# Rebuilding the first stages of a product-quantised convolution block and issuing three lookups ahead of the numerators

## The chip, the cores and the metric

The kernel runs on one core of one Trainium2 chip. The metric is the device time of one execution in microseconds (us), median over runs. Ratios are computed as the mean time of one kernel's runs over that of the other's of the same rounds, so they are not quite the ratios of the medians quoted.

## The reference, cut to what matters

x is 16 images of 256 channels of 28 x 28, fp32. Twice in a row each channel's 3 x 3 patches are compared with 16 centroids, and a softmax over them weighs a table of 256 outputs:

```python
def amm_conv3x3(x, centroids, w_sub):
    p = patches(x)                                    # B, 784, C, 9
    d = sum(p*p) - 2*einsum('bncs,cks->bnck', p, centroids) + sum(centroids**2)
    attn = softmax(-d)                                # over 16 centroids
    lut = einsum('cks,cso->cko', centroids, w_sub)
    return einsum('bnck,cko->bno', attn, lut)

out = relu(bn1(amm_conv3x3(groupnorm(x), centroids1, wsub1)))
out = se(bn2(amm_conv3x3(out, centroids2, wsub2)))
return x + relu(out + groupnorm(x))
```

## The kernel before: the parts that the change and the argument touch

The work is 512 steps: 16 images x 2 layers x 2 halves of the pixels (384 and 400) x 8 groups of 32 channels. A step has these parts: **logits** (16 small matmuls of patches and codes on TensorE), **exponentials** (two activations on ScalarE), **numerators** (16 small matmuls), two **transposes** and a reciprocal on VectorE, the product with the reciprocal on GpSimd, one more transpose, and, three steps later, the **lookups** (matmuls of 128 x 128 with the sub-weights; 36 for 8 steps). Patches come from DRAM: each normalised image is written there in nine shifted copies and read back as rows.

Eight PSUM banks are two accumulators and three pairs that rotate:

```python
def pair():
    turn[0] += 1
    return ring[turn[0] % 3]

def logits(u, rows):
    ps = [pair(), pair()]
    for t in range(4):
        for i in range(4):
            nc.tensor.matmul(ps[t // 2][...], lhsT=wd..., rhs=u["pt"]..., ...)

def b_exp(u):      # ScalarE: two activations of 2 x 400
    for ps in u.pop("lg"):
        nc.scalar.activation(e[:, :, :n], ps[:, :, :n], AF.Exp, scale=2.0)

def b_num(u):
    u["nm"] = [pair(), pair()]
    ...            # t = 0, 1 need the first exponential, t = 2, 3 the second

def b_turn(u):     # VectorE: frees the numerators' pairs
    for v, ps in enumerate(u.pop("nm")):
        nc.vector.transpose(nt[...2 * v...], ps[...])
    nc.vector.reciprocal(rc[...], u["nt"][:, :, SUM])
```

A pair is two banks, and holds half of a group's results. Four pairs are taken per step and three exist. If a step's logits have pairs a and b, its numerators have c and a, and the next logits have b and c. So the **second half of the next logits waits for the first transpose of this step's numerators**.

Within a step the order on every engine is by position:

```python
LOGITS, LOAD, MOVE, EXP, LOOK_A, NUM, TURN, SMALL, LOOK_B, MAX, LOOK_C, TURN_BACK, REST = range(13)
...
for i, (m, o, h) in enumerate(LOOKS[k : k + n]):
    self.at(s, LOOK_A if i < n // 2 + n % 2 - more[q] // 2 else LOOK_B if i < n - more[q] else LOOK_C, c_look, ...)
```

n is 4 or 5; it is 2 more in steps in which an extra group of logits for a maximum is made (position MAX). SMALL holds tiny matmuls of the group statistics and of the gate.

Before the loop, image 0 is normalised and written out. The channels are sorted by an estimate of their range, and the first layer's sub-weights are sorted with them on TensorE. The second layer's tables are sorted during the first steps.

## Time and profile before

| | before |
|---|---|
| median of 3 runs | 2973.09 us (2972.99 to 2977.15) |
| span of the profiled run | 2969.2 us |
| TensorE idle in the first 80 us | 47.1 us |
| first logits | 57.0 us |
| numerators after two lookups, width 384 / 400 | 1.04 / 1.19 us |
| logits of the same size | 0.86 / 0.88 us |

A start-to-start distance (from a group's start to the next group's) is the right measure of a group here, since a busy TensorE is not one at its peak. Two lines of the list of waits of the kernel before (who waited for whom: us in total, times, longest) name the wait that the numerators have and the one that logits nearly never had. L631 are the numerators, L563 the logits, PEld is the weight load in front of a matmul.

```profile
PEld pair L631 <- ACT e L621: 321.4, 555, 7.1
...
PEld pair L563 <- DVE nt L643: 7.4, 11, 1.2
```

The totals are idle time of the weight loads. Most of it overlaps matmuls, so the counts tell more than the microseconds: 555 waits for exponentials against 11 for transposes.

### The profile page before, as it was taken

What the parts mean: (1) busy time and instruction counts of PE and PEld (TensorE: products, weight loads), DVE (VectorE), ACT (ScalarE), POOL (GpSimd) and SP (SyncE); (2) the same over time, 40 slices, a digit from 0 to 9 for tenths busy, and PEclk for the clock granted to TensorE, in tenths of its full rate; (3) what the DMA queues carried; (4) which work ended last, traced back from release to release, by engine and by line L of the source; (5) the groups of instructions that cost most, each with busy time, mean ns of one, the idle gap of its engine ahead of it and who ended that gap; (6) DMA issues with size and microseconds to landing.
All of it is one profiled execution on the core that took longest, in us unless ns stands there. A gap on an engine that the chain in (4) does not pass through costs nothing.

```text
span 2969.2 us, 94838 instructions
## 1 busy us (share of the span) xinstructions
PE 2871.6 (97%) x39834; PEld 1145.4 (39%) x39834; DVE 2252.7 (76%) x2760; ACT 1092.7 (37%) x1605; POOL 1768.5 (60%) x2583
## 2 busy tenths in 40 slices
PE   4999999999999999999999999999999999999995
PEld 2433333333333333333333333333333333334332
DVE  3476777787877878787787877878788787878884
ACT  1332343433434343343433434343343434333332
POOL 3474575666656566665656656566665656656553
PEclk8999999999999999999999999999999999999998
DMA  6877777767767676776767667676776767674641
GB/s 185 227 174 170 203 219 195 212 154 213 186 169 197 151 208 174 197 185 154 211 156 207 180 180 188 154 214 156 214 185 163 200 155 206 177 189 106 163 114 56
DMA packets 296773, 530.30 MB, mean 179 GB/s; under 512 B 94240, under 2 KB 251664, under 8 KB 296336
## 3 DMA queue, kind: packets, MB, share of 16 engines
q0 software_dynamic: 51648, 269.78, 34.9%
q1 hardware_dynamic: 242512, 251.70, 32.7%
q8 instruction: 316, 5.18, 0.7%
q10 hardware_dynamic: 2176, 2.65, 0.3%
q14 instruction: 121, 0.99, 0.1%
HBM read 269.96 MB, written 254.05 MB: 176 GB/s over the span
## 4 chain that ended last, share of the span: by engine, by line
PE 79%; DMA 7%; DVE 6%; POOL 4%; issue 2%; ACT 2%; SPq 0%; ACTq 0%; DVEq 0%; POOLq 0%
PE acc L695 47%; PE pair L631 16%; PE pair L563 14%; DMA xt<-in_x 4%; DVE nt L643 2%; POOL k L659 2%; DVE rc L649 1%; DVE gn_st L417 1%; POOL total L671 1%; DMA pt<-pat 1%; ACT e L621 1%; DMA ws<-dws 1%; PE pair L309 0%; PE pair L324 0%; DVE q L677 0%
## 5 line engine op out<-in xcount | busy, mean ns | idle before, releaser
L695 PE MATMUL acc<-q,ws 128*128 128x384 f32 (+1 forms) x4096 | 1641.0, 519 | 9.7 <-ACT y L717 9.7
L659 POOL TENSOR_TENSOR k<-nt,rc 128x832 f32<-128x832 f32 (+1 forms) x512 | 802.3, 1567 | 1132.9 <-DVE rc L649 1120.5
L643 DVE STREAM_TRANSPOSE nt<-pair 128x832 f32<-128x832 f32 (+1 forms) x1024 | 976.3, 992 | 603.5 <-PE pair L631 506.4
L621 ACT ACTIVATE e<-pair 128x800 f32<-128x800 f32 (+1 forms) x1024 | 787.8, 821 | 1358.8 <-PE pair L563 1357.3
L695 PEld LDWEIGHTS acc<-q,ws 128*128 128x128 f32 x4096 | 696.9, 189 | 907.7 <-issue 577.2
L631 PE MATMUL pair<-e,cw 32*32 32x384 f32 (+1 forms) x16384 | 580.3, 502 | 11.9 <-ACT e L621 10.6
L563 PE MATMUL pair<-pt,wd 19*32 19x384 f32 (+2 forms) x18432 | 561.0, 500 | 5.9 <-DMA pt<-pat 3.3
L677 DVE STREAM_TRANSPOSE q<-k 128x832 f32<-128x832 f32 (+1 forms) x512 | 489.1, 955 | 0.8 <-POOL k L659 0.8
L649 DVE RECIPROCAL rc<-nt 128x104 f32<-128x104 f32 (+1 forms) x512 | 398.5, 778 | 17.6
L631 PEld LDWEIGHTS pair<-e,cw 32*32 32x32 f32 x16384 | 167.5, 103 | 349.2 <-ACT e L621 321.4
L563 PEld LDWEIGHTS pair<-pt,wd 19*32 19x32 f32 (+1 forms) x18432 | 138.4, 103 | 340.1 <-issue 265.5
L665 POOL TENSOR_TENSOR tail<-nt,rc 128x104 f32<-128x104 f32 (+1 forms) x512 | 242.4, 473 | 0.0
L695 PE MATMUL acc<-qt,ws 128*128 128x400 f32 (+1 forms) x512 | 218.6, 509 | 0.0
L671 POOL TENSOR_TENSOR total<-total,nt 128x96 f32<-128x96 f32 (+1 forms) x448 | 198.7, 443 | 0.0
L468 POOL DMA_DIRECT2D pat<-side x280 | 186.6, 667 | 1.1 <-DMA pat<-im 0.7
L671 POOL TENSOR_TENSOR total<-total,rc 128x96 f32<-128x96 f32 (+1 forms) x448 | 175.5, 392 | 0.0
L695 PEld LDWEIGHTS acc<-qt,ws 128*128 128x128 f32 x512 | 90.8, 189 | 100.1 <-issue 50.6
L587 DVE TENSOR_REDUCE mx<-z 128x48 f32<-128x768 f32 (+1 forms) x128 | 120.8, 943 | 0.0
L582 DVE STREAM_TRANSPOSE z<-pair 128x768 f32<-128x768 f32 (+1 forms) x128 | 119.2, 969 | 0.0
L468 POOL DMA_DIRECT2D pat<-im x140 | 94.0, 672 | 3.5 <-ACT im L447 3.5
L707 ACT ACTIVATE im<-acc,bnsh,bnsc 128x384 f32<-128x384 f32 (+1 forms) x64 | 43.4, 678 | 139.4 <-PE acc L695 133.4
L717 ACT ACTIVATE y<-acc,bnsh,bnsc 128x384 f32<-128x384 f32 (+1 forms) x64 | 43.4, 679 | 91.7 <-PE acc L695 76.8
(106 smaller groups left out, 753.5 us busy)
## 6 DMA issues: line engine op xcount, KB each, us to landing
pat<-side POOLq DMA_DIRECT2D x232, 588.0 KB, 6.1
pt<-pat SPq DMA_DIRECT2D x1024, 112.5 KB
pt<-pat SPq DMA_DIRECT2D x1024, 108.0 KB
pat<-im POOLq DMA_DIRECT2D x116, 588.0 KB, 5.3
xt<-in_x POOLq DMA_DIRECT2D x32, 784.0 KB, 8.8
out_dram<-y POOLq DMA_DIRECT2D x16, 784.0 KB, 4.0
pat<-side POOLq DMA_DIRECT2D x24, 300.0 KB, 6.1
pat<-side POOLq DMA_DIRECT2D x24, 288.0 KB, 6.0
```

Source lines behind the costliest of these rows:

```text
L468: nc.gpsimd.dma_start(view(pat, (ROWS * p0 + 9 * k + 3 * dx) * HW + px, [[ROWS * HW, m], [HW, 3], [1, n]]), bass.AP(v.tensor, v.offset, [l ...
L563: nc.tensor.matmul(ps[t // 2][c : c + 32, t % 2, :n], lhsT=wd[l][32 * i : 32 * i + rows, 4 * u["m"] + t, :], rhs=u["pt"][32 * i : 32 * i + ...
L587: nc.vector.tensor_reduce(u["mx"][:, 2 * v : 2 * v + 2].rearrange("p t (j b) -> p t b j", j=2)[:, :, :nb], u["z"].pop(0)[:, : 64 * nb].rea ...
L621: nc.scalar.activation(e[:, :, :n], ps[:, :, :n], AF.Exp, scale=2.0)
L631: nc.tensor.matmul(u["nm"][t // 2][32 * i : 32 * i + 32, t % 2, :n], lhsT=cw[l][c : c + 32, 4 * u["m"] + t, :], rhs=es[t // 2][c : c + 32, ...
L643: nc.vector.transpose(nt[:, :nb, 2 * v : 2 * v + 2].rearrange("p b t r -> p t b r"), ps[:, :, : 32 * nb].rearrange("p t (b r) -> p t b r", ...
L649: nc.vector.reciprocal(rc[:, : 8 * nb], u["nt"][:, :, SUM])
L659: nc.gpsimd.tensor_tensor(q[:, :nb].rearrange("p b (a s) -> p (b a) s", s=8), nt[:, :, :8], rc.unsqueeze(2).to_broadcast([P, 8 * nb, 8]), ...
L665: nc.gpsimd.tensor_tensor(tails[key][:, :nb, 8 * (m % 4) : 8 * (m % 4) + 8], nt[:, :, 8].rearrange("p (b a) -> p b a", a=8), rc.rearrange( ...
L671: nc.gpsimd.tensor_add(t[:, : 8 * nb], t[:, : 8 * nb], v)
L677: nc.vector.transpose(q[:, :, : 32 * nb].rearrange("p h (b r) -> p h b r", r=32), u.pop("k")[:, :nb].rearrange("p b (h r) -> p h b r", h=2),)
L695: nc.tensor.matmul(accs[key][:, :n], lhsT=ws[l][:, 2 * m + h if h < 2 else 2 * NQ + m // 4, o * P : (o + 1) * P], rhs=u["q"][h][:, :n], st ...
```

## The change

Its intent is to start the loop earlier and to give the exponentials time for one more lookup before the numerators need them. The channel sort moves to where x loads. The first layer's sub-weights are loaded at once into three of the six patch buffers. Patch writes go by the first half of the channels, then the second. The second layer's sorted sub-weights are copied by VectorE, and its sorted tables (codes and sub-weights) are stored by GpSimd. In the loop, three lookups always go ahead of the numerators.

```diff
+    raw = [t.rearrange("p a n -> p (a n)")[:, :1536]... for t in pts[3:]]
+    for i in range(NLT * P // PART):
+        nc.sync.dma_start(raw[i // 2][:, i % 2], ws1[:, i * PART : (i + 1) * PART]...)
...
-            nc.scalar.dma_start(view(d_c2[i], ...), t)
+            nc.gpsimd.dma_start(view(d_c2[i], ...), t)
...
-        nc.scalar.copy(r, ps[:, :, :PART])
-        nc.scalar.dma_start(view(d_ws2, ...), r)
+        nc.vector.tensor_copy(r, ps[:, :, :PART])
+        nc.gpsimd.dma_start(view(d_ws2, ...), r)
...
-    STEPS = [(dx, k, h) for dx in (1, 0, 2) for k in range(NB) for h in range(2)]
+    STEPS = [(dx, k, h) for h in range(2) for dx in (1, 0, 2) for k in range(NB)]
...
-                        self.at(s, LOOK_A if i < n // 2 + n % 2 - more[q] // 2 else LOOK_B if i < n - more[q] else LOOK_C, c_look, of[m], o, h)
+                        self.at(s, LOOK_A if i < 3 else LOOK_B if i < n - more[q] else LOOK_C, c_look, of[m], o, h)
...
-                    self.at(t + 4 * i + 2 + k, REST, shift, l, dx, k)
+                    self.at(t + (2 * i + k if pace == 1 else i), REST, shift, l, dx, k)
...
+    bn_setup()
+    row = sort_keys()
+    square_codes(0)
     for k in range(NB):
         gn_stats(0, k)
     gn_mean(0)
     gn_var(0)
+    sort_ranks(row)
+    setup_codes(0)
...
-            n0 = -3 if b == 1 else t - 2 * NS - 3
+            n0 = 2 if b == 1 else t - 2 * NS - 3
```

Cut here: the order of loads, the second issuer (SyncE) of the first patch writes, the arithmetic of the slots of the patch writes, and the removal of what moved.

More of the change, by code (lines that the diff above doesn't have):

```diff
@@ L24 @@
 NQ = NT // 4
+PART = 384
 NLT = NQ * 9 // 4
@@ L150 @@
     load_x(0, x[0])
-    pts = [const.tile([P, 4, 400], F32, name=f"pt{i}") for i in range(6)]
-    for t in pts:
-        nc.sync.dma_start(t[ONE::32], view(consts, 0, [[0, 4], [0, 4], [1, 400]]))
     def load(ap, name):
@@ L163 @@
     vecs = load(vec, "vecs")
-    nhalf_sb = load(nhalf, "nhalf_sb")
-    mones_sb = const.tile([P, 2, 32], F32, name="mones_sb")
-    nc.sync.dma_start(mones_sb, mones.rearrange("l p m -> p l m"))
     c2_sb = const.tile([P, NB, K * 9], F32, name="c2_sb")
@@ L177, with ones_row @@
     perm = sort_sb[:, n_in : n_in + NB * C].rearrange("p (b c) -> p b c", b=NB)
+    nhalf_sb = load(nhalf, "nhalf_sb")
     wd = [load(wd1, "wd0"), const.tile([P, NT, 32], F32, name="wd1")]
+    mones_sb = const.tile([P, 2, 32], F32, name="mones_sb")
+    nc.sync.dma_start(mones_sb, mones.rearrange("l p m -> p l m"))
+    pts = [const.tile([P, 4, 400], F32, name=f"pt{i}") for i in range(6)]
+    def ones_row(t):
+        nc.sync.dma_start(t[ONE::32], view(consts, 0, [[0, 4], [0, 4], [1, 400]]))
+    for t in pts[:3]:
+        ones_row(t)
+    raw = [t.rearrange("p a n -> p (a n)")[:, :1536].rearrange("p (i b m) -> p i b m", i=2, b=NB) for t in pts[3:]]
+    for i in range(NLT * P // PART):
+        nc.sync.dma_start(raw[i // 2][:, i % 2], ws1[:, i * PART : (i + 1) * PART].rearrange("(b p) m -> p b m", p=P))
     cw = [load(cw1, "cw0"), load(cw2, "cw1")]
@@ L240, in scratch, with sort_keys @@
         return kpool.tile([P, 13, 64], F32, tag="k", name="scratch").rearrange("p i m -> p (i m)")[:, :n]
-    def sort_channels():
+    def sort_keys():
         sc, sh = bn[0]
@@ L263, in sort_channels, with sort_ranks @@
         nc.vector.tensor_copy(row, ps[:, :C])
+        return row
+    def sort_ranks(row):
         own = small.tile([P, NB], F32, name="key_own")
@@ L292, in sort_bn @@
             nc.vector.tensor_copy(bn[0][i], ps[:, i : 2 * NB : 2])
-    PART = 384
     parts = {}
@@ L303, in sort_ws1 @@
     def sort_ws1(i):
-        t = parts.pop(i)
+        t = raw[i // 2][:, i % 2]
         for j in range(PART // P):
@@ L339, in sort_c2 @@
                 )
-            nc.scalar.dma_start(view(d_c2[i], 0, [[K * 9, P], [P * K * 9, NB], [1, K * 9]]), t)
+            nc.gpsimd.dma_start(view(d_c2[i], 0, [[K * 9, P], [P * K * 9, NB], [1, K * 9]]), t)
     def sort_ws2(i):
@@ L346, in sort_ws2 @@
         r = tpool.tile([P, 832], F32, tag="z", name="part")[:, : NB * PART].rearrange("p (b m) -> p b m", b=NB)
-        nc.scalar.copy(r, ps[:, :, :PART])
-        nc.scalar.dma_start(view(d_ws2, i * PART, [[9 * C, P], [P * 9 * C, NB], [1, PART]]), r)
+        nc.vector.tensor_copy(r, ps[:, :, :PART])
+        nc.gpsimd.dma_start(view(d_ws2, i * PART, [[9 * C, P], [P * 9 * C, NB], [1, PART]]), r)
     def place_wd2(j, s):
@@ L459, in shift, with to_pat @@
             nc.scalar.copy(to[:, :, 0 : W - 1], img[:, :, 1:W])
-    STEPS = [(dx, k, h) for dx in (1, 0, 2) for k in range(NB) for h in range(2)]
-    def to_pat(l, i, pat, px=0, n=HW):
+    STEPS = [(dx, k, h) for h in range(2) for dx in (1, 0, 2) for k in range(NB)]
+    def to_pat(l, i, pat, px=0, n=HW, eng=nc.gpsimd):
         dx, k, h = STEPS[i]
@@ L467, in to_pat @@
         v = (ims[l] if dx == 1 else sides[dx])[p0 : p0 + m, k, px:]
-        nc.gpsimd.dma_start(
+        eng.dma_start(
             view(pat, (ROWS * p0 + 9 * k + 3 * dx) * HW + px, [[ROWS * HW, m], [HW, 3], [1, n]]),
@@ L791, in stage, with prep, prep_near @@
                 self.tiles.append((n0, of))
-        def prep(self, l, pat, t):
+        def prep(self, l, pat, t, pace=1):
             for i, dx in enumerate((0, 2)):
                 for k in range(NB):
-                    self.at(t + 4 * i + 2 + k, REST, shift, l, dx, k)
+                    self.at(t + (2 * i + k if pace == 1 else i), REST, shift, l, dx, k)
             for i in range(len(STEPS)):
-                self.at(t + i, REST, to_pat, l, i, pat)
-        def prep_near(self, l, pat, t, slots, t2, slots2):
+                self.at(t + int(i * pace), REST, to_pat, l, i, pat)
+        def prep_near(self, l, pat, t):
             for i, dx in enumerate((0, 2)):
@@ L805, in prep_near @@
                     self.at(t + i, REST, shift, l, dx, k)
-            for i in range(len(STEPS)):
-                self.at(t + i * slots // len(STEPS), REST, to_pat, l, i, pat, *PXT[0])
-                self.at(t2 + i * slots2 // len(STEPS), REST, to_pat, l, i, pat, *PXT[1])
+            n = len(STEPS) // 2
+            for i, (dx, k, h) in enumerate(STEPS):
+                self.at(t + i // 2, REST, to_pat, l, i, pat, *PXT[0])
+                self.at(t + 6 if dx == 1 else t + 7 + 3 * h + (i - n * h - NB) * 3 // 4, REST, to_pat, l, i, pat, *PXT[1])
         def norm(self, b, t):
@@ L847 @@
             shift(0, dx, k)
-        to_pat(0, i, d_pat[0], *PXT[0])
-    square_codes(0)
-    setup_codes(0)
-    bn_setup()
-    sort_channels()
+        to_pat(0, i, d_pat[0], *PXT[0], eng=nc.gpsimd if dx == 0 or (dx, h) == (1, 1) else nc.sync)
     sort_bn()
@@ L859 @@
         if l == 0 and b >= 1:
-            n0 = -3 if b == 1 else t - 2 * NS - 3
-            plan.at(n0 - 2, REST, load_x, b, x[b])
+            n0 = 2 if b == 1 else t - 2 * NS - 3
+            plan.at(n0 - (6 if b == 1 else 2), REST, load_x, b, x[b])
             plan.norm(b, n0)
-            plan.prep(0, pat_of(0, b), {1: 1, 2: 32, 3: 56}.get(b, t - 2 * NS + 3))
+            plan.prep(0, pat_of(0, b), {1: 8, 2: 33, 3: 57}.get(b, t - 2 * NS + 3), 0.7 if b == 1 else 1)
         if l == 1:
             if b in (0, B - 1):
-                t0 = t - NS + LC
-                plan.prep_near(1, pat_of(1, b), t0, 4, t0 + 4, 8)
+                plan.prep_near(1, pat_of(1, b), t - NS + LC)
             else:
-                plan.prep(1, pat_of(1, b), 44 if b == 1 else t - 2 * NS + LC + 1)
+                plan.prep(1, pat_of(1, b), 45 if b == 1 else t - 2 * NS + LC + 1)
             plan.at(t + NS, REST, load_x, b, x[b])
@@ L872 @@
     for i in range(len(STEPS)):
-        plan.at(i // 3, REST, to_pat, 0, i, d_pat[0], *PXT[1])
-    n1 = NLT * P // PART
-    for i in range(n1):
-        if i < 2:
-            plan.at(-6, REST, load_part, ws1, i)
-            plan.at(-1, REST, sort_ws1, i)
-        else:
-            plan.at((i - 2) * 3 // 4 - 1, REST, load_part, ws1, i)
-            plan.at((i - 2) * 3 // 4, (LOOK_A, LOOK_B)[i % 2], sort_ws1, i)
+        plan.at(i * 5 // len(STEPS), REST, to_pat, 0, i, d_pat[0], *PXT[1])
+    for i in range(NLT * P // PART):
+        plan.at((i - 2) // 2, REST if i < 2 else (LOOK_A, LOOK_B)[i % 2], sort_ws1, i)
+        if i % 2:
+            plan.at((i - 2) // 2, REST, ones_row, pts[3 + i // 2])
     plan.at(3, REST, sort_c2)
```

## The prediction

> **What bounds the kernel now.** I read the profile's first two parts, then the table of stretches, then TensorE's instructions in order of time, early and in the middle.
>
> ```profile
> PE 2871.6 (97%) x39834; PEld 1145.4 (39%) x39834; DVE 2252.7 (76%) x2760; ACT 1092.7 (37%) x1605; POOL 1768.5 (60%) x2583
> ```
>
> TensorE is busy for all but 2969.2 - 2871.6 = 97.6 us. The stretches of the start (length, then busy time and count for each engine, granted clock, DMA share, GB/s) say where nearly half of that lies:
>
> ```profile
> 0.00:20.00 20.00, 1.17 (x4) 1.00 (x4) 4.11 (x22) 5.12 (x8) 7.13 (x21) 1.00 0.57 174
> 20.00:40.00 20.00, 4.97 (x10) 2.76 (x10) 8.43 (x28) 1.34 (x2) 10.22 (x17) 0.85 0.90 273
> 40.00:60.00 20.00, 13.72 (x75) 10.78 (x76) 6.45 (x21) 3.43 (x8) 0.38 (x2) 0.63 0.44 108
> 60.00:80.00 20.00, 13.03 (x190) 6.78 (x189) 7.18 (x11) 5.86 (x11) 10.96 (x20) 0.88 0.77 199
> 80.00:100.00 20.00, 19.61 (x215) 9.90 (x207) 11.22 (x14) 7.58 (x12) 13.26 (x22) 0.95 0.90 252
> ```
>
> TensorE does 32.9 us in the first 80, so it idles 47.1. The first logits start at 57.01. They wait behind one serial chain: statistics of x at 9.8, patch writes from 17.8, the code squares behind those writes in GpSimd's order (26.3), VectorE's channel sort (33.5 to 43.1), the statistics of the second batch (45.4), then 8.34 us of sub-weight sorting on TensorE. At the end 9.7 us are one wait of the last stage for the previous output's store, and some 21 us are the tail. Both stay.
>
> The rest is a steady loop of 512 steps, one for four matmul groups: 16 logits, lookups, 16 numerators, lookups. A timeline of TensorE in it (start, us, line, count; fp32 matmuls are counted twice, so x4 is two lookups):
>
> ```profile
> 1516.05 0.93 PE L563 MATMUL pair<-pt,wd 21*32 21x384 f32 x32
> 1516.91 1.61 PE L695 MATMUL acc<-q,ws 128*128 128x400 f32 x4
> 1518.45 1.08 PE L631 MATMUL pair<-e,cw 32*32 32x384 f32 x32
> 1519.47 1.61 PE L695 MATMUL acc<-q,ws 128*128 128x400 f32 x4
> 1521.01 0.93 PE L563 MATMUL pair<-pt,wd 19*32 19x384 f32 x32
> ```
>
> From one group's start to the next: logits 0.86, two lookups 1.54, numerators 1.02. Logits and numerators have the same size, so the numerators lose 0.16 here. I took this distance for all groups between 400 and 2880 us. Where two lookups stand ahead and nothing special happens, numerators take 1.04 at width 384 (106 groups) and 1.19 at 400 (115); where three stand ahead, mostly 0.86 and 0.88. The exponentials explain it: ScalarE starts 1.04 us after the logits' start and needs 0.75 to 0.83 each for two, so the second ends 0.1 to 0.3 us after the numerators have started. This loss is counted as busy.
>
> **What the Trainium skill says.** "Perfetto Trace Analysis", section "Identifying the Most-Contended Engine", says that matmul busy time is no good measure of the distance to the roofline. This trace agrees: the 97% contain the numerators' loss of some 0.24 us per affected step. "TensorE: Matmul & The Clock Gate", section "Architectural detail: the array is 16× 32×32, not 1× 128×128", gives TensorE a queue in which weight loads are pulled ahead of running matmuls, while ScalarE and VectorE are strict FIFO. The trace agrees in what a wait costs: if the second half of a group is released late, the whole half, 0.84 us, follows the release instead of half of 0.88. One case in full:
>
> ```profile
> 890.13 0.90 PE L563 MATMUL pair<-pt,wd 19*32 19x400 f32 x16
> 890.29 1.94 DVE L643 STREAM_TRANSPOSE nt<-pair 128x832 f32<-128x832 f32 x2
> 891.35 0.91 PE L563 MATMUL pair<-pt,wd 19*32 19x400 f32 x16 [0.32 <-DVE nt L643]
> 892.18 1.27 PE L695 MATMUL acc<-q,ws 128*128 128x400 f32 x3
> ```
>
> The first transpose ends at 890.29 + 0.97 = 891.26, 1.13 after the logits' start; the group takes 2.05. The logits that were held by a transpose ending 0.37, 0.43, 0.47, 0.61, 1.00 and 1.13 after their start took 1.30, 1.37, 1.39, 1.53, 1.92 and 2.05. So a group takes (release after its start) + 0.93, and at least 0.86 to 0.88. Lastly "DMA: Bandwidth & Descriptors", section "Issuing engines are not separate DMA queues", says that all issuers share the same 16 engines; splitting the writes over two issuers therefore saves issue time (0.65 us each on GpSimd here), not bandwidth.
>
> **The change, part by part.**
> (1) *Start.* The sort's keys run while x loads, the ranks during the normalisation, the squares before it. From the durations in the trace: x lands at about 10, but its statistics now stand behind the keys on VectorE (3.8 us of work plus a 0.45 MB load), so I put them at 12.5 to 14.7; normalised x at 20 (16.5 to 18.5 before); ranks 15 to 21, code setup to 24, sort of the batch norm to 26; sub-weight sorting 26 to 33 because the weights are already in patch buffers. Patch writes start at 20, and the first patches need only the first half of channels, 1.8 of 3.5 MB. But 2.4 MB of sub-weights now load before, about 8 us at the 273 to 340 GB/s seen at this place; so the first patches land at about 33. First logits at 34 instead of 57: -23. Steps 0 to 3 took 57 to 84 us with two stalls, 6.4 us on ScalarE (held by normalising batch 1, which now moves to steps 6 and 7) and about 2 on VectorE; I take -6 for them and give 2 back to crowded DMA (share 0.90 at 80 to 100). Sum: -27 us.
> (2) *Weight copies and their DMA issues* go from ScalarE to VectorE and GpSimd: six of under 1 us, beside other work, 0.
> (3) *Three lookups ahead.* By the loop's plan a pair of stages (32 steps) has 22 steps with four lookups, 2 of four lookups plus two that go with a maximum, and 8 that had three ahead already. So 352 and 32 steps change from 2+2 to 3+1, and from 2+2+2 to 3+1+2. About 40 of the 352 have a tiny matmul of the statistics or of the gate in between and neither gain nor lose much, leaving 310.
>  Gain: the numerators' excess goes: 1.04 - 0.86 = 0.18 and 1.19 - 0.885 = 0.305, mean 0.24.
>  Loss: three PSUM pairs rotate, four are taken per step, so the second half of the next logits gets the numerators' first pair, and must wait until VectorE has transposed it. That transpose starts 1.05 (384) or 1.08 (400) after the numerators' start, with two and with three lookups ahead alike, and lasts 0.93 or 0.99: released at 1.98 or 2.07. With two lookups behind, the logits start at about 2.6: free. With one they start at 0.86 + 0.745 = 1.60 or 0.88 + 0.77 = 1.65; the release comes 0.38 or 0.42 after, so they take 1.31 or 1.35 instead of 0.86 or 0.88: +0.46.
>  Net 310 x (0.46 - 0.24) = +68. In the 32 maximum steps the extra logits lose the 0.46, and the logits after them wait for the first maximum transpose (ends 4.75 after the numerators' start, they start at about 4.5: +0.27): 32 x (0.73 - 0.24) = +16. Sum +84, of which I take 3 as hidden in the crowded first stage: +81.
> Total: 2973 - 27 + 81 = 3027 us, 1.8% slower.
>
> **Rivals.**
> (a) The wait on the transpose does not replace the wait on the exponential, say because the logits' start moves for another reason. Then 310 + 32 steps gain 0.24, -82, and with the start -109: 2864 us. For it: steps with three ahead show numerators at the floor. Against it: all those have two lookups behind, so they say nothing of one behind; and the rotation and the six releases above are direct.
> (b) The start gains nearly nothing, since DMA becomes its bound: bytes up to 100 us are 20.1 MB at a mean of 201 GB/s, and the share is 0.90 at 20 to 40. Then 3045 to 3054 us. Against it: the DMA share is 0.44 at 40 to 60, when TensorE sorts, so there is room.
> (c) VectorE, 76% busy, becomes the bound in steps with maxima: its backlog starts the transpose later than 1.08 (1.35 in a tenth of steps), adding up to 0.3 to a tenth of 310, +9: 3036.
>
> **Range and chances.** Rival (a) I give 8%; it is the only way to faster by over 2% (under 2914). Otherwise start -15 to -33 and loop +60 to +100 give 3000 to 3058 about 3027. The limit of slower by over 2% is 3033, just above my middle, hence 39%.
>
> **What would show it.** Right: first logits near 34 us; numerators at 0.86 to 0.88 after three lookups; logits after a single lookup at 1.3 to 1.35, with TensorE waiting for the transposes into nt; waits of numerators for the exponentials gone. Wrong: logits still at 0.88 (then a), first logits after 45 (then b), transposes starting more than 1.1 after the numerators (then c).

## The result, and the profile after

The changed kernel takes **3014.0 us** (median of 3, 3012.25 to 3018.08) against 2973.09. The ratio is 1.0136, interval 1.0113 to 1.0159. So it is 41 us, 1.4%, slower, which counts as the same within 2%. The prediction said 3027, 54 us slower, with a range of 3000 to 3058.

In the changed kernel's source the lines are 10 further down: L573 logits, L641 numerators, L653 the transposes, L705 lookups. The same stretches of the start as the prediction shows for before (length, busy time and count of PE, PEld, DVE, ACT, POOL, granted clock, DMA share, GB/s):

```profile
0.00:20.00 20.00, 2.75 (x9) 2.28 (x10) 12.96 (x54) 1.60 (x3) 8.06 (x21) 1.00 0.86 278
20.00:40.00 20.00, 11.27 (x38) 8.06 (x37) 4.06 (x10) 6.34 (x10) 5.99 (x11) 0.83 0.77 187
40.00:60.00 20.00, 15.68 (x148) 8.67 (x164) 3.73 (x6) 5.02 (x10) 4.41 (x7) 0.74 0.49 143
60.00:80.00 20.00, 18.92 (x266) 9.16 (x235) 15.23 (x22) 6.39 (x12) 13.88 (x22) 1.00 0.87 236
80.00:100.00 20.00, 15.98 (x165) 7.26 (x165) 10.33 (x13) 4.22 (x6) 12.62 (x23) 0.95 0.65 180
```

TensorE is busy 48.6 us of the first 80 instead of 32.9: VectorE now sorts in the first 20 us (12.96 busy, 4.11 before). But from 80 to 100 TensorE stands for 4.0 us, before for 0.4. The first logits start at 44.22 us instead of 57.01:

```profile
44.22 3.72 PE L573 MATMUL pair<-pt,wd 19*32 19x384 f32 x32 [10.80 <-issue]
```

The loop, in order of time, TensorE and VectorE (start, us, line, count):

```profile
1545.86 0.93 PE L641 MATMUL pair<-e,cw 32*32 32x384 f32 x32
1546.72 0.91 PE L705 MATMUL acc<-q,ws 128*128 128x384 f32 x2
1546.91 1.85 DVE L653 STREAM_TRANSPOSE nt<-pair 128x768 f32<-128x768 f32 x2 [2.26 <-PE pair L641]
1547.56 1.27 PE L573 MATMUL pair<-pt,wd 21*32 21x384 f32 x32
1548.76 2.20 PE L705 MATMUL acc<-q,ws 128*128 128x384 f32 x6
...
1550.89 0.93 PE L641 MATMUL pair<-e,cw 32*32 32x384 f32 x32
```

Read the distances: numerators 0.86 (1.02 in the prediction's excerpt), one lookup 0.84, logits 1.20 (0.86 before), three lookups 2.13. The first transpose ends at 1546.91 + 0.92 = 1547.83, that is 0.27 after the logits' start, and 0.27 + 0.93 = 1.20. The weight loads of those logits name the reason in brackets:

```profile
1547.56 0.18 PEld L573 LDWEIGHTS pair<-pt,wd 21*32 21x32 f32 x16 [0.55 <-DMA pt<-pat]
1547.95 0.18 PEld L573 LDWEIGHTS pair<-pt,wd 21*32 21x32 f32 x16 [0.21 <-DVE nt L653]
```

The second 16 weight loads start only after the transpose. The list of waits turned round accordingly:

```profile
PEld pair L573 <- DVE nt L653: 95.8, 340, 2.2
PEld pair L641 <- ACT e L631: 88.9, 158, 1.7
```

Logits waited for transposes 340 times instead of 11, numerators for exponentials 158 times instead of 555.

**Where the time went.** VectorE makes one reciprocal per step, so their 512 start times in each trace align the two runs step by step. Changed minus before: -9.0 us at step 0, -17.0 at step 4, -9.6 at step 7, -10.5 at step 16; then it rises steadily, to -1.2 at step 128, +9.6 at 256, +23.1 at 384, and +40.6 at the last step. So the start (here up to step 16) gained 10.5 us, and the loop lost 51.1 us over 495 steps.

### The profile page after: what moved, and what is told of

Its sections match the earlier page's. It is cut to its first block, busy times and chain, and to the rows that moved or that the text cites. A ratio compares the mean times of both kernels' runs of the same rounds, so it can differ in the third digit from the quotient of the medians.

```text
span 3010.4 us, 94911 instructions
## 1 busy us (share of the span) xinstructions
PE 2908.8 (97%) x39834; PEld 1148.4 (38%) x39834; DVE 2258.3 (75%) x2766; ACT 1095.1 (36%) x1599; POOL 1767.6 (59%) x2585
## 4 chain that ended last, share of the span: by engine, by line
PE 87%; DMA 4%; POOL 3%; DVE 3%; issue 2%; SPq 0%; ACT 0%; DVEq 0%; POOLq 0%; ACTq 0%
PE acc L705 52%; PE pair L573 20%; PE pair L641 14%; DMA xt<-in_x 3%; POOL k L669 1%; DVE nt L653 1%; POOL total L681 1%; DVE rc L659 1%; PE pair L319 1%; PE pair L334 1%; POOL tail L675 0%; DVE gn_st L427 0%; DMA pt<-dm 0%; DMA pat<-im 0%; PE pair L506 0%
## 5 line engine op out<-in xcount | busy, mean ns | idle before, releaser
L705 PE MATMUL acc<-q,ws 128*128 128x384 f32 (+1 forms) x4096 | 1647.7, 521 | 17.1 <-ACT y L727 9.8
L653 DVE STREAM_TRANSPOSE nt<-pair 128x832 f32<-128x832 f32 (+1 forms) x1024 | 977.2, 992 | 635.0 <-PE pair L641 461.6
L705 PEld LDWEIGHTS acc<-q,ws 128*128 128x128 f32 x4096 | 695.7, 190 | 927.5 <-issue 589.8
L573 PE MATMUL pair<-pt,wd 19*32 19x384 f32 (+2 forms) x18432 | 690.3, 501 | 22.9 <-issue 10.8
L641 PE MATMUL pair<-e,cw 32*32 32x384 f32 (+1 forms) x16384 | 487.1, 500 | 1.0 <-ACT e L631 1.0
L573 PEld LDWEIGHTS pair<-pt,wd 19*32 19x32 f32 (+1 forms) x18432 | 187.0, 103 | 437.6 <-issue 256.6
L641 PEld LDWEIGHTS pair<-e,cw 32*32 32x32 f32 x16384 | 121.3, 103 | 289.9 <-issue 176.2
L705 PE MATMUL acc<-qt,ws 128*128 128x400 f32 (+1 forms) x512 | 215.0, 502 | 0.0
L705 PEld LDWEIGHTS acc<-qt,ws 128*128 128x128 f32 x512 | 93.6, 190 | 88.3 <-issue 28.9
```

Source lines behind the costliest of these rows:

```text
L573: nc.tensor.matmul(ps[t // 2][c : c + 32, t % 2, :n], lhsT=wd[l][32 * i : 32 * i + rows, 4 * u["m"] + t, :], rhs=u["pt"][32 * i : 32 * i + ...
L641: nc.tensor.matmul(u["nm"][t // 2][32 * i : 32 * i + 32, t % 2, :n], lhsT=cw[l][c : c + 32, 4 * u["m"] + t, :], rhs=es[t // 2][c : c + 32, ...
L653: nc.vector.transpose(nt[:, :nb, 2 * v : 2 * v + 2].rearrange("p b t r -> p t b r"), ps[:, :, : 32 * nb].rearrange("p t (b r) -> p t b r", ...
L705: nc.tensor.matmul(accs[key][:, :n], lhsT=ws[l][:, 2 * m + h if h < 2 else 2 * NQ + m // 4, o * P : (o + 1) * P], rhs=u["q"][h][:, :n], st ...
```

## The experiments

All ran with five rounds beside the kernel before, and all were correct. Where two experiments are compared ("4.3 us better than"), the figure is the difference of their medians if they ran on the same chip beside the same runs of the kernel before, and otherwise the difference of their differences to it. First the two halves of the change, each alone.

### The loop's line alone

```diff
 (kernel before)
-  LOOK_A if i < n // 2 + n % 2 - more[q] // 2 else LOOK_B if ...
+  LOOK_A if i < 3 else LOOK_B if ...
```

> The kernel before with one line changed: three lookups ahead of the numerators, the start left as it was. Theory (the loop lost, the start gained): aligned by step, the changed kernel lost 51 us from step 16 to step 511, so this one should take 2973 + 51 = 3024 us (3015 to 3032), with numerators at 0.86 to 0.88 us and logits after a single lookup at about 1.2 to 1.29 us. Rival (the loss comes from the new start, for instance from weights or batches that arrive later and push every later step): this one stays within 10 us of 2973, or gets faster, since the numerators no longer wait.

Measured: 3015.59 us against 2971.05, ratio 1.0156 (1.0138 to 1.0173). That is 44.5 us slower, at the low edge of what was expected. Numerators took 0.86 and 0.91 us, logits after a single lookup 1.20 and 1.25. The loop's one line is enough for the whole loss, and the rival falls. Aligned by steps this run loses 5.7 us up to step 16 and 38.6 after it, so some 12 of the 51.1 us that the changed kernel lost in its loop are not this line's alone; the part on the prediction comes back to most of them.

### The new start alone

```diff
 (changed kernel)
-  LOOK_A if i < 3 else LOOK_B if ...
+  LOOK_A if i < n // 2 + n % 2 - more[q] // 2 else LOOK_B if ...
```

> The changed kernel with the old split of the lookups (two, or three of five, ahead) and its new start. Theory: 2973 minus the 10 to 12 us that the changed kernel was ahead at step 16, so 2958 to 2966 us, and numerators back at 1.04 and 1.19 us. Rival (start to blame): above 3000 us.

Measured: 2954.06 us, ratio 0.9948 (0.9934 to 0.9961), 17.0 us faster. That is more than expected. The alignment by steps shows why: the lead is 5.2 us at step 80 and grows to 19.2 by the end, so the rewritten patch writes help in the loop as well. Those writes need shifted image copies on ScalarE, and the change moves these copies to other steps. In the kernel before, one stood right in front of the exponentials in two of every 32 steps (timeline of TensorE and ScalarE):

```profile
957.54 0.98 PE L563 MATMUL pair<-pt,wd 19*32 19x400 f32 x32
...
958.64 0.81 ACT L459 COPY side<-im 128x756 f32<-128x756 f32 x1
959.36 1.56 ACT L621 ACTIVATE e<-pair 128x800 f32<-128x800 f32 x2
960.24 1.63 PE L631 MATMUL pair<-e,cw 32*32 32x400 f32 x32 [0.18 <-ACT e L621]
```

The numerators of such a step take 1.56 us. From step 72 to 499, outside the steps with tiny matmuls, the kernel before has 26 numerators over 1.3 us, 25 of them in these two steps of each 32; with the new start alone there are 4. The mean at width 400 falls from 1.19 to 1.12.

The two halves sum to +44.5 - 17.0 = +27.5, but together they measured +41. Some 11 of the 14 us are counted twice in the sum: with three lookups ahead a late exponential costs nothing, so moving the copies gains nothing there. In the plain steps (four lookups and nothing extra) of width 400, where the copies were in the way, the line alone cost 12.2 us from step 72 to 499, the new start alone saved 13.0, and both together cost 10.5.

### The keys' row in its own buffer

```diff
 (new start alone)
-  row = tpool.tile([P, 832], F32, tag="z", name="row")[:, :C]
+  row = const.tile([P, C], F32, name="row")
```

> As the start alone, and the row of sort keys gets a buffer of its own. In the changed kernel the third square of the codes waits on GpSimd until 17.30 us for a buffer of the rotation that the row still holds, and the deviations of the statistics, next in GpSimd's order, run at 18.11 where their input was ready at 13.99. Theory: normalising starts at about 18 instead of 21.6 us, the first logits 3 to 4 us earlier, and the time falls by 2 to 4 us against the start alone. Rival: the transfers that load sub-weights (until about 18 us) hold the patch writes anyway; then the first logits come less than 1 us earlier and the time does not move.

Measured: 2949.73 us, ratio 0.993 (0.9916 to 0.9944), 4.3 us better than the new start alone; the first logits came at 40.8 instead of 44.1 us. GpSimd in the changed kernel had shown the wait:

```profile
9.65 1.61 POOL L399 TENSOR_TENSOR sq<-wd 128x384 f32<-128x384 f32 x2 [3.07 <-DMA wd<-in_wd]
17.30 0.85 POOL L399 TENSOR_TENSOR sq<-wd 128x256 f32<-128x256 f32 x1 [6.03 <-DVE scratch L286]
18.11 0.37 POOL L437 TENSOR_TENSOR gn_dv<-gn_mv,gn_gm 128x2 f32<-128x2 f32 x1
```

With the row apart the deviation (`gn_dv`) runs at 14.08 us. The intervals of the two ratios overlap slightly. The first logits and the wait leave no doubt about the mechanism at the start: at step 12 the row apart is still 3.3 us ahead of the start alone (-17.1 against -13.8 us). But then the traced runs lose a lead that differs from one to the next, from step 12 to 16: 9.0 us with the start alone, 2.2 here, 5.2 and 5.4 in the runs with x later and with the old order below. Why was not followed, so differences of a few us between the medians of these runs say little by themselves.

### The stores issued from ScalarE again

```diff
 (the row apart)
-  nc.gpsimd.dma_start(view(d_c2[i], ...), t)
+  nc.scalar.dma_start(view(d_c2[i], ...), t)
...
-  nc.gpsimd.dma_start(view(d_ws2, ...), r)
+  nc.scalar.dma_start(view(d_ws2, ...), r)
```

> As the run with the row apart, and the stores of the sorted second-layer tables are issued from ScalarE again instead of GpSimd. In the changed kernel steps 6 to 7 gave back 7 us: a store issued by GpSimd only at 88.12 us, behind its multiplications, landed at about 93, only then was the buffer free for the next part of sub-weights, which landed at 99.15, and TensorE stood for it. Theory: with the old issuer this wait shrinks and the time falls by 4 to 7 us against the run with the row apart. Rival: the copy on VectorE, not the issue, is what comes late, or ScalarE gets as late by issuing; then no more than 1 us is gained.

Measured: 2961.85 us, ratio 0.9969 (0.9956 to 0.9982), 12 us worse than the row apart. The rival was right that nothing is gained, but neither of its reasons is what the trace shows. The lead over the kernel before, 20 us at step 4 in both runs, is 20.3 at step 5 with GpSimd as the issuer and 10.5 with ScalarE. There TensorE stands for a part of the sub-weights, whose load SyncE issued late (the first line is from the run with the row apart, the others from this one):

```profile
64.72 1.19 SPq L310 DMA_DIRECT2D part<-in_wsub  x1
...
78.28 0.42 SPq L310 DMA_DIRECT2D part<-in_wsub  x1
...
83.50 5.10 PE L334 MATMUL pair<-part,sort_sb 128*128 128x384 f32 x8 [7.39 <-DMA part<-in_wsub]
88.53 0.93 PE L573 MATMUL pair<-pt,wd 19*32 19x384 f32 x32
...
90.17 1.51 ACT L631 ACTIVATE e<-pair 128x768 f32<-128x768 f32 x2 [15.25 <-DVE part L357]
```

In front of that load, SyncE's order has loads of patches, and one of them waited for the store of a sorted code table that ScalarE issued only at 70.31 us (list of waits, 55 to 95 us):

```profile
SPq L560 <- DMA dc<-scratch: 13.8, 2, 13.6
```

The load and the store signal their end on the same semaphore (a counter that instructions wait for; number 108 in the trace). With GpSimd as the issuer the stores use others (102 and 103), and this wait is not there. ScalarE stands for 15.25 us as well, because its next store waits for VectorE's copy of the part and the exponentials come behind it. But the logits that these exponentials read start only at 88.53, and elsewhere the exponentials start 1.04 us after the logits, so this cost some 0.6 us. All this is read from one trace, that of the fastest of the five runs (2951.40; the others 2959.81 to 2964.51). Its lead at the end is 19.1 us against 24.9 with the row apart, so it does not show the whole of the 12.

### Numerators one step behind

To take away both waits without a new buffer in PSUM, each step's numerators go behind the next step's logits:

```diff
 (the row apart)
-  epool = ... tile_pool(name="epool", bufs=2)
+  epool = ... tile_pool(name="epool", bufs=4)
...
-  at(s, NUM, b_num, u)
-  at(s, TURN, b_turn, u)
-  at(s, TURN, c_scale, u)
-  at(s + 1, TURN_BACK, c_turn, u)
+  at(s + 1, NUM, b_num, u)
+  at(s + 1, TURN, b_turn, u)
+  at(s + 1, TURN, c_scale, u)
+  at(s + 2, TURN_BACK, c_turn, u)
```

and lookups, the closing of an image and the preparation of the next one step later.

> As the run with the row apart (two lookups ahead, two behind), but each step's numerators are issued one step later, behind the next step's logits, with four buffers for the exponentials and the lookups one step later too. Then the numerators' exponentials are a whole step old, and the logits' second pair is released by a transpose that is two lookups and a group of numerators old. Theory (both losses are these two waits): numerators and logits all at 0.86 to 0.88 us; a plain step falls by 0.18 us at width 384 and by about 0.24 at 400, 305 of them, and the time by 55 to 75 us to 2875 to 2895. Rival: numerators are slow for a reason of their own (the switch between groups, their weights), or VectorE, 83% of a step at the new pace, becomes the bound: then less than 25 us are gained.

Measured: **2888.84 us** against 2971.7, ratio 0.9735 (0.9718 to 0.9752): faster than both kernels, by 82.9 us against before and 62 against the row apart. Numerators took 0.857 and 0.884 on plain steps, logits 0.86 to 0.90:

```profile
1501.42 0.93 PE L573 MATMUL pair<-pt,wd 19*32 19x384 f32 x32
1502.28 1.56 PE L705 MATMUL acc<-q,ws 128*128 128x384 f32 x4
1503.76 0.93 PE L641 MATMUL pair<-e,cw 32*32 32x384 f32 x32
1504.62 1.56 PE L705 MATMUL acc<-q,ws 128*128 128x384 f32 x4
```

Both groups now take the same 0.86. Its start is worse than that of the row apart (lead 5.9 us at step 16 instead of 14.9); the loop gives the rest.

### Numerators one step behind, three lookups ahead

```diff
 (numerators one step behind)
-  LOOK_A if i < n // 2 + n % 2 - more[q] // 2 else LOOK_B if ...
+  LOOK_A if i < 3 else LOOK_B if ...
```

> As the lagging numerators, with three lookups ahead and one behind. No numerators wait in either of the two, so the difference to the lagging run with two and two is the cost of the wait on the transpose alone. Theory: the logits after a single lookup take 1.19 (384) and 1.28 us (400) as in the changed kernel, +0.33 and +0.40 on 305 plain steps, +0.45 on 34 with a maximum: 100 to 130 us slower than the lagging run. Rival (the single lookup, or the order of the lookups itself, costs): the logits stay at 0.86 to 0.88 and the difference is under 40 us or lies in the lookups.

Measured: 3020.07 us, ratio 1.0167 (1.0153 to 1.018), 131 us slower than with two and two. This is the clean price of the wait on the transpose, since here the numerators have nothing to gain: the logits after a single lookup take about 1.27 us again and the weight loads wait for it,

```profile
PEld pair L573 <- DVE nt L653: 92.7, 346, 1.8
```

as often as in the changed kernel (340).

### One lookup ahead

```diff
 (the row apart)
-  LOOK_A if i < n // 2 + n % 2 - more[q] // 2 else LOOK_B if ...
+  LOOK_A if i < 1 else LOOK_B if ...
```

> As the run with the row apart, with one lookup ahead of the numerators and three or four behind. By the rule of the prediction (a group takes its release after its start plus 0.93): the second exponential ends 2.55 (384) to 2.7 us (400) after the logits' start, the numerators start 0.86 + 0.85 = 1.71 after it, so they take 1.77 to 1.92 us instead of 1.04 and 1.12, and nothing is gained behind them: +0.73 to +0.8 on some 340 steps and more on those with three ahead before, 250 to 380 us slower, near 3260. Rival (numerators are slow for a reason of their own): they take 1.1 to 1.3 us and the time rises by under 80.

Measured: 3271.14 us, ratio 1.101 (1.0995 to 1.1024), 321 us slower than the row apart. Numerators take 1.51 (384) and 1.56 us (400), and the lookup ahead 1.03 and 1.08 where one takes 0.85, because the numerators' very start now waits too. Per plain step that is +0.66, a little under the +0.73 expected. That the numerators' time follows the exponentials, from 0.86 to 1.56 with nothing else changed, rules out a slowness of their own.

### The second batch of x later

```diff
 (the row apart)
-  plan.at(n0 - (6 if b == 1 else 2), REST, load_x, b, x[b])
+  plan.at(n0 - 2, REST, load_x, b, x[b])
```

> As the run with the row apart, but the second batch of x (0.8 MB), issued at 28.5 us in the changed kernel, is issued four steps later, after the first logits. Theory (the first patches wait for shared DMA bandwidth, 200 to 290 GB/s at 24 to 44 us): the first logits come about 3 us earlier, and the time falls by up to 3 us. Rival (the patches wait for latency and order of the writes, not for bandwidth): first logits within 1 us of before.

Measured: 2950.42 us, ratio 0.9929 (0.9915 to 0.9943), the same as the row apart. The first logits did come 2.2 us earlier (38.6), so bandwidth does hold the first patches. In the trace the lead was lost again at step 6 (-16.7 against -16.3 us), where both wait.

### Sub-weight parts in their own buffers

```diff
 (the row apart)
-  t = tpool.tile([P, 832], F32, tag="z", name="part")...
+  t = wpool.tile([P, NB * PART], F32, tag="w", name="part")...     # wpool: two buffers
```

> As the run with the row apart, and the parts of the second layer's sub-weights load into two buffers of their own instead of the rotation of three that they share with their sorted copies. In the run with the row apart the lead over the kernel before falls from 20 to 16 us at step 6, in the changed kernel from 16 to 10 at step 7, each time with TensorE standing for a part. Theory (the parts are late because their buffer waits for the store of the previous sorted part): the lead stays near 20 us through step 12, and the time falls by 3 to 4 us against the run with the row apart. Rival: the sorted copies still wait for the stores in the same rotation, or bandwidth holds the parts: no change within 1.5 us.

Measured: 2945.0 us against 2968.5, ratio 0.9915 (0.9901 to 0.9928), 2.2 us better than the row apart, with overlapping intervals. The theory falls: the lead drops from 22.6 us at step 5 to 18.5 at step 6 as before. In this stretch it is GpSimd that stands, for the store of another buffer, and what it computes next is late for TensorE. From the run with the row apart:

```profile
81.63 1.50 POOL L669 TENSOR_TENSOR k<-nt,rc 128x768 f32<-128x768 f32 x1 [5.07 <-DMA dc<-scratch]
...
84.49 0.20 POOL L438 TENSOR_TENSOR gn_dv<-gn_dv 128x2 f32<-128x2 f32 x1
...
84.74 0.38 PE L444 MATMUL pair<-gn_dv,gmat 128*128 128x2 f32 x2 [2.43 <-POOL gn_dv L438]
```

That the changed kernel's own loss at step 7 has the same cause is not shown; there TensorE stood 3.3 us for a part of the sub-weights.

### The first writes in the old order

```diff
 (the row apart)
-  for i, (dx, k, h) in enumerate(STEPS):
+  for i in sorted(range(len(STEPS)), key=lambda i: ((1, 0, 2).index(STEPS[i][0]), STEPS[i][1:])):
+      dx, k, h = STEPS[i]
```

> As the run with the row apart, but the first batch's first patch writes go in the old order, in which the first patches need eleven of the twelve writes instead of six. Theory (the half of the channels brings the first patches forward): the first logits come 3 to 6 us later than 40.8. Rival (all writes, the second batch of x and the reads share the engines until 44 us anyway, so that the order hardly matters): under 1.5 us.

Measured: 2947.96 us, ratio 0.9927 (0.9913 to 0.994), the same; first logits at 40.3 instead of 40.8 us. The reads of the first patches were issued at 37.5 instead of 31.7 us, yet landed no later. Writing half of the channels first brings nothing at the start. This fits the rival, that writes and reads share the bandwidth until all have passed; no run tests that reason by itself.

## Why the prediction was right

Direction, range and mechanism held; the sizes of two terms did not, and they erred in opposite directions: the start gained 16.5 us less than said and the loop lost 30 less. That the total came within 13 us is partly luck.

- **The loop loses because a wait on the transpose takes the place of the wait on the exponential.** Shown by the loop's line alone (+44.5 us), by the turned list of waits, and by numerators one step behind: without either wait the loop takes some 80 us less than before from step 16 on (10 of them the row apart has too), and the transpose's wait put back costs 131.
- **The gain of the numerators** was taken as 0.18 and 0.305 us; they fell from 1.04 to 0.86 and from 1.19 to 0.88.
- **The loss of the logits** was taken as 0.46. It measured 0.33 (0.86 to 1.20) at 384 and 0.41 (0.88 to 1.29) at 400. The rule "release plus 0.93" held; the term mis-sized was the single lookup in front, taken as half of two (0.745 and 0.77), which measured 0.85 and 0.86 (means over plain steps). The logits start later and the release comes sooner after them. The three lookups ahead save what the single one costs (2.16 instead of 2.25), so all lookups together take the same.
- **The sum of the loop** was +81 and measured +51. The means by kind of step, from steps 72 to 499, give it back: 305 plain steps with four lookups at +0.15 (384) or +0.08 (400), together +34 where the prediction had +68; 34 with a maximum at +0.29 or +0.38, +11 where it had +16. The steps with tiny matmuls were put at no effect: 44 of them fell by 0.40 or 0.26, -16, and 14, in which TensorE now stands for a result of GpSimd, rose by 0.88, +12. Plain steps with five lookups at width 400 rose by 0.21, about +10, and this is not the third lookup's doing: they had it before. The logits after one such step in 32 take up to 3.2 us, because VectorE's statistics of the next image wait for its x from DRAM and stand in front of the transposes. In the changed kernel, after logits whose first half started at 2148.19:

```profile
2148.27 1.04 DVE L427 BATCH_NORM_STATS2 gn_st<-xt 128x6 f32<-128x392 f32 x2 [2.94 <-DMA xt<-in_x]
...
2150.53 0.91 PE L573 MATMUL pair<-pt,wd 19*32 19x400 f32 x16 [1.44 <-DVE nt L653]
```

The prediction's case at 890 us is one of these. How late x comes differs from run to run: against the kernel before, these steps cost +8.1 us from step 72 to 499 in the changed kernel and -1.5 in the loop's line alone, and with the old split of the lookups -0.6 (the start alone), +3.6 (the row apart) and +8.3 (the old order).
- **The start** was put at -27 us and gained 10.5. The step that failed is "the first patches land at about 33; first logits at 34": they came at 44.2, so 12.8 us were gained there instead of 23. The 4 us put on the first steps came to nothing either: the lead was 17.0 at step 4 and 10.5 at step 16. For the late patches two causes are shown. Normalising began at 21.6 instead of 20, because a square of the codes waited for a buffer (worth 3.3 us at the first logits, the row apart). And the term that only half of the writes count is void (old order: no later); at the 273 GB/s of the prediction the other 1.7 MB are 6 us, an estimate. The prediction's rival (b), DMA as the bound, was right for the first patches, with the second batch of x worth 2.2 us; its time, 3045 to 3054, was not reached because the loop lost less.
- **The copies and issues moved off ScalarE** were put at 0 as a removal from ScalarE. With the copy on VectorE, the issue on ScalarE would have cost 12 us, at least in part for the wait on SyncE that it brought.
- **Missing altogether**: the shifted copies that moved away from the exponentials, worth 13 us in the loop with two lookups ahead (plain steps of width 400: -13.0 with the start alone, -13.2 with the row apart). No run moves them alone; it is the place of the gain and the slow numerators there that point to them.
- Rival (c) did not come: on plain steps the transposes start 1.05 and 1.08 us after the numerators, mean 1.06 and 1.10 (1.10 and 1.13 before). Late ones (over 1.2 us) are fewer, from step 72 to 499 27 instead of 79, and 12 of the 27 are those behind the statistics.

## What to carry to other kernels

When you give one engine more slack by moving work ahead of a wait, look at what that work was hiding on the other side: with a rotation of buffers, every group stands between two releases, and moving one lookup took more from one (0.33 and 0.41 us) than it gave to the other (0.18 and 0.305). If the slack cannot be had on both sides, lag one of the groups by a whole step: two more buffers for the exponentials in SBUF made it 2.7% faster where no split of the lookups did. And measure a short run of instructions before you scale it: one lookup alone is not half of two.

## What the Trainium skill lacked or had wrong

- "TensorE: Matmul & The Clock Gate" tells of the queue that pulls weight loads ahead, and the trace agrees (in the kernel before, a lookup's weights load from 885.93 us, while the lookup in front runs until 886.43). It does not tell what a late release costs: a group of 16 small fp32 matmuls in 4 x 4 tiles takes 0.86 to 0.88 us, and when its second half is released late it takes the release after its start plus 0.93 us (1.20 with a release at 0.27, 2.05 at 1.13). So a release at 0.43, when half of the group is through, already costs some 0.5 us (1.37), and by this sum the margin must be about half a group, an estimate.
- No page that we read gives the time of a short run of fp32 matmuls of 128 x 128 between small ones: one takes 0.84 us, two 1.49, three 2.13 at width 384, some 0.65 each and 0.2 per run.
- "DMA: Bandwidth & Descriptors", section "Issuing engines are not separate DMA queues", weighs the choice of the issuing engine by the issue time alone. Here it also decided what another engine's loads waited for: with the stores issued by ScalarE, SyncE stood 13.6 us for one of them, a part of the sub-weights was loaded at 78.28 instead of 64.72 us, and TensorE stood 7.39 us for it.
